# Four states of a selective scan: one scanned in PSUM, one on DVE and three on POOL multiplied by C, the sums over the states as matmuls with an identity

## The chip, the cores and the metric

The kernel runs on one core of one Trainium2 chip. The metric is the device time of one execution in microseconds (us). Before the change it is 11720.34 us, the median of three runs (11690.25 to 11727.8).

The engines are named as the profile names them: PE is TensorE's matmul, PEld its weight load, DVE is VectorE, ACT is ScalarE, POOL is GpSimd, SP is SyncE, which issues the DMAs. PE, DVE, ACT and POOL each run their instructions in the order in which the program wrote them.

## What is computed

An image batch of shape (4, 64, 64, 96) passes through four layers. Layers 0 and 1 are two-dimensional selective scans (1 works on the Fourier transform of the image), layers 2 and 3 are attention and a quantized feed-forward network over tokens. The scans take nearly all of the time. For each of four directions k, each channel d and each of 16 states n, along the sequence l:

```
delta = softplus(dt_w @ dts + dt_b)            # per direction, channel, position
h[d,n]  = h[d,n] * exp(delta[d] * A[d,n]) + delta[d] * u[d] * B[n]
y[d]    = sum_n h[d,n] * C[n]  + Ds[d] * u[d]
y_out   = y_0 + flip(y_2) + transpose(y_1 + flip(y_3))
```

Then `y_out` is layer-normalized, gated with silu(z) and projected. B and C depend on the position but not on the channel; delta and u depend on the channel but not on the state.

## The kernel before

**Tiling.** Channels lie on the 128 partitions, the sequence on the free axis. Each block of layers has C = 3 chunks of 128 channels. Layer 0 (`CFG0`) packs two images with 64 channels each into a chunk (NI = 2, PI = 64); its two image pairs are two phases. Layer 1 (`CFG1`) has one image and 128 channels per chunk (NI = 1, PI = 128), so four phases. Each direction of a phase is cut into segments: eight of 512 positions in layer 0, and 512, 512, 384, 384 and 320 in layer 1. That gives 64 segments in layer 0 and 80 in layer 1. A segment is done in 12 steps: for q in 0..3 (four states each) and c in 0..2 (chunk). So there are 768 steps in layer 0 and 960 in layer 1.

**One step** (the loop from L763) makes four scans on DVE (`scan`, L660, `tensor_tensor_scan`): state 0 and 1 of the four go to the tile `hx`, state 2 and 3 to `hy`. Their coefficients exp(delta*A) are made by ACT (`exp`, L635): for states 0 and 1 into SBUF (`ax`, `front_x`), for 2 and 3 into PSUM (`front_y`). The inhomogeneous term delta*u*B comes in two ways. For states 0 and 1, ACT scales the transposed delta*u by B, one number per partition (`make_bx`, L600), and PE transposes the result back into PSUM (`transposed`, L630). For states 2 and 3, POOL multiplies delta*u by a B that a DMA has spread over all partitions (`front_b`, L653, tile `hy`). The products with C are made by POOL for `hx` (L805, both states in one instruction of 2S elements, S being the segment's length) and by DVE for `hy` (L822, both states in one instruction). The sum over the states is made by PE: `accumulate` (L682) transposes each 128x128 block of each product into the accumulator `acc` with `is_transpose=True`, so that the sum lies with positions on the partitions. `keep_state` (L673) keeps the last column of each scan for the next segment: POOL for `hx`, mostly ACT for `hy`.

**PSUM** has eight banks: three accumulators, three "ab" rooms, through which the four PSUM tiles of a step (two transposed B terms, two exps) rotate, one bank "pp" for the preparation of the next segment, one bank "ms" for all side work.

**Order.** Scans run under a manual schedule. In the gaps (`slot`, three a step) `prepare` (projections, softplus, transposes of the next segment) and a queue of side tasks (`E.step`: the convolution and projections of the next phase, the gating of the last one) are advanced a piece at a time; `rate` (1.75 to 2.5 pieces a step) limits the side tasks. `burst` places softplus and silu. So a matmul that waits on PE holds all matmuls behind it, the scan's and the side tasks'.

**After a segment,** `close_chunk` copies `acc` (ACT) and stores it to DRAM, positions first. `gated` (from L352) reads the four directions back, two rows of the image at a time, and adds them in PSUM: three plain matmuls with the diagonal of the summed Ds (`skip`, L397) and twelve transposes (L403) for each two rows.

## Time and profile before

The profiled execution has a span of 11704.4 us, 0.14% under the median of the runs (11720.34 us).

| | |
|---|---|
| span of the profiled execution | 11704.4 us |
| median of the runs | 11720.34 us (11690.25 to 11727.8) |
| busy: PE / PEld | 9301.7 (79%) / 6722.3 us |
| busy: DVE | 10549.4 us (90%) |
| busy: ACT | 9089.0 us (78%) |
| busy: POOL | 8931.5 us (76%) |
| mean granted PE clock | 0.880 |
| DMA | 1469.07 MB, 126 GB/s, queue share 45.5% |
| head before the first scan / stretch of the scans / tail | 0 to 218, 218 to 11313, 11313 to 11704 us |

The busy share of an engine is time in which at least one of its instructions was in flight. For PE this is more than the time that its array was needed: consecutive matmuls overlap, and a single one is shown for some 0.27 us although the next can start 0.11 us later. So the work of PE is better counted by the distance from the start of one instruction to the start of the next, where nothing holds them. The groups of instructions give, for a line and a shape, the count, the busy time, the mean duration of one, and what the engine waited for before them; a plain fp32 matmul is two instructions in them, a transposing one is one.

### The profile page before, as it was taken

The page shows a single profiled execution, that of the slowest core. Times are in us where ns is not written, and L with a number is a line of the kernel's source. Part 1 is how long each engine was busy: PE and PEld are TensorE (multiplying, and loading weights), DVE is VectorE, ACT ScalarE, POOL GpSimd, SP SyncE. Part 2 cuts the span into 40 slices and gives each one's busy share as a digit, 9 for nine tenths or more (in the row PEclk, how much of TensorE's full clock was granted, in tenths as well). Part 3 has the DMA queues.
Part 4 walks back from the last instruction along what each step waited for, and adds up shares of the span by engine and source line. Part 5 has one row for each costly group of instructions (what it writes and reads, how often), then busy time and mean ns, then how long its engine had stood idle before and what let it go on. Part 6 is the DMA issues. An engine that isn't in the chain of part 4 may idle for free. (4 is left out here: it accounts for less than half of the span.)

```text
span 11704.4 us, 164864 instructions
## 1 busy us (share of the span) xinstructions
PE 9301.7 (79%) x54800; PEld 6722.3 (57%) x54800; DVE 10549.4 (90%) x10183; ACT 9089.0 (78%) x18533; POOL 8931.5 (76%) x7075
## 2 busy tenths in 40 slices
PE   6678888787888878877888888888778877788765
PEld 3455555555666556555665565565556655565554
DVE  6899999999999998999888989988999999899974
ACT  3778888898888888887767878877787787777753
POOL 2889999887887897897768878877767767677640
PEclk8789999988988998998889989988879988898887
DMA  5454454555555445445544353454225432443242
GB/s 145 120 142 119 126 127 115 141 155 158 153 153 129 124 124 141 120 127 162 153 129 124 114 147 120 142 150 119 88 79 158 122 96 92 124 137 106 83 117 42
DMA packets 1270879, 1469.07 MB, mean 126 GB/s; under 512 B 496071, under 2 KB 1033871, under 8 KB 1260679
## 3 DMA queue, kind: packets, MB, share of 16 engines
q1 hardware_dynamic: 1270023, 1458.53, 45.5%
q8 instruction: 430, 7.05, 0.3%
q14 instruction: 426, 3.49, 0.1%
HBM read 1221.74 MB, written 236.50 MB: 125 GB/s over the span
## 5 line engine op out<-in xcount | busy, mean ns | idle before, releaser
L653 POOL TENSOR_TENSOR hy_l<-du_l,bc_l 128x512 f32<-128x512 f32 (+2 forms) x3456 | 3957.3, 1166 | 1934.8 <-DVE hcy_l L822 960.1
L805 POOL TENSOR_TENSOR hcx_l<-hx_l,bc_l 128x1024 f32<-128x1024 f32 (+2 forms) x1617 | 3525.5, 2180 | 239.1 <-DVE hx_l L660 197.9
L600 ACT ACTIVATE bx_l<-dut_l,bt_l 128x192 f32<-128x192 f32 (+2 forms) x6272 | 2793.7, 498 | 0.0
L682 PE MATMUL acc_l<-ident,hcx_l 128*128 128x128 f32 (+1 forms) x12006 | 1876.0, 305 | 392.6 <-POOL hcx_l L805 388.4
L635 ACT ACTIVATE ax_l<-delta_l,l_alog 128x512 f32<-128x512 f32 (+2 forms) x3456 | 2139.1, 667 | 0.0
L682 PE MATMUL acc_l<-ident,hcy_l 128*128 128x128 f32 (+1 forms) x12000 | 1841.9, 302 | 302.4 <-DVE hcy_l L822 299.0
L682 PEld LDWEIGHTS acc_l<-ident,hcy_l 128*128 128x128 f32 (+1 forms) x12000 | 1551.5, 155 | 859.2 <-DVE hcy_l L822 475.7
L682 PEld LDWEIGHTS acc_l<-ident,hcx_l 128*128 128x128 f32 (+1 forms) x12006 | 1526.4, 156 | 861.5 <-POOL hcx_l L805 665.9
L822 DVE TENSOR_TENSOR hcy_l<-hy_l,bc_l 128x1024 f32<-128x1024 f32 (+2 forms) x1616 | 1951.1, 1207 | 43.6
L660 DVE TENSOR_TENSOR_SCAN hx_l<-ax_l,state_l,b_l 128x512 f32<-128x512 f32 (+2 forms) x1650 | 1787.4, 1124 | 212.7 <-PE b_l L630 136.9
L660 DVE TENSOR_TENSOR_SCAN hy_l<-b_l,state_l,hy_l 128x512 f32<-128x512 f32 (+2 forms) x1649 | 1782.9, 1118 | 89.3 <-ACT b_l L635 81.4
L635 ACT ACTIVATE b_l<-delta_l,l_alog 128x512 f32<-128x512 f32 (+2 forms) x1913 | 1196.6, 628 | 627.6 <-DVE hx_l L660 599.0
L630 PE MATMUL b_l<-ident,bx_l 128*128 128x128 f32 (+1 forms) x6724 | 1169.6, 302 | 363.0 <-DVE hy_l L660 203.5
L635 ACT ACTIVATE ab_l<-delta_l,l_alog 128x512 f32<-128x512 f32 x1321 | 907.1, 689 | 547.5 <-DVE hx_l L660 496.4
L630 PEld LDWEIGHTS b_l<-ident,bx_l 128*128 128x128 f32 (+1 forms) x6724 | 827.1, 152 | 861.3 <-DVE hy_l L660 337.1
L660 DVE TENSOR_TENSOR_SCAN hy_l<-ab_l,state_l,hy_l 128x512 f32<-128x512 f32 x961 | 1172.1, 1257 | 60.8 <-POOL hy_l L653 31.9
L660 DVE TENSOR_TENSOR_SCAN hx_l<-ax_l,state_l,ab_l 128x512 f32<-128x512 f32 x962 | 1176.5, 1263 | 49.3 <-PE ab_l L630 27.3
L630 PE MATMUL ab_l<-ident,bx_l 128*128 128x128 f32 x5288 | 889.1, 305 | 383.2 <-DVE hy_l L660 206.3
L673 POOL COPY state_l<-hx_l 128x2 f32<-128x2 f32 x1344 | 1141.9, 850 | 0.0
L630 PEld LDWEIGHTS ab_l<-ident,bx_l 128*128 128x128 f32 x5288 | 652.0, 154 | 715.6 <-DVE hy_l L660 326.6
L274 PE MATMUL pc_l<-pad_l,l_dg 128*128 128x512 f32 (+2 forms) x1656 | 787.9, 564 | 56.0 <-ACT uh_l L252 46.6
L176 PE MATMUL pi_l<-xi_l,l_wi 96*128 96x384 f32 (+6 forms) x912 | 458.6, 619 | 180.0 <-ACT zh_l L342 60.4
(225 smaller groups left out, 11821.3 us busy)
## 6 DMA issues: line engine op xcount, KB each, us to landing
bc_l<-l_xd_l SPq DMA_DIRECT2D x1536, 256.0 KB
bc_l<-l_xd_l SPq DMA_DIRECT2D x384, 512.0 KB
bc_l<-l_xd_l SPq DMA_DIRECT2D x384, 384.0 KB
us_l<-l_u SPq DMA_DIRECT2D x96, 768.0 KB
l_y<-y_l SPq DMA_DIRECT2D x288, 256.0 KB
bc_l<-l_xd_l SPq DMA_DIRECT2D x192, 320.0 KB
yt_l<-l_y SPq DMA_DIRECT2D x264, 192.0 KB
yt_l<-l_y SPq DMA_DIRECT2D x128, 384.0 KB
```

Source lines behind the costliest of these rows:

```text
L176: self.nc.tensor.matmul(out[i * cfg.PI : (i + 1) * cfg.PI, :n], wi[:, ki, half, :], xin[:, max(i, ki), :n], start=(ki == 0), stop=(ki == c ...
L274: nc.tensor.matmul(pc[:, : n * 64].rearrange("p (r w) -> p r w", w=64), diag[:, t, :], pad[:, r - p0 + dy : r - p0 + dy + n, dx : dx + 64] ...
L600: nc.scalar.activation(t[:n, b, :, ch], z.dut[:n, b, :, ch], AF.Copy, scale=z.bt[:n, b, m : m + 1])
L630: nc.tensor.transpose(pb[:, t : t + n], st.z.bx[st.q, j][:n, b, st.c], ident[:n, :n])
L635: nc.scalar.activation(out, z.delta[:, st.c, : z.S], AF.Exp, scale=z.blk.A[:, st.c, z.k, n : n + 1])
L653: nc.gpsimd.tensor_tensor(st.hy[:, j, :S], st.z.du[:, st.c, :S], st.z.b[st.q][:, j, :S], ALU.mult)
L660: nc.vector.tensor_tensor_scan(h[:, j, : z.S][:, ::step], a[:, : z.S][:, ::step], b[:, : z.S][:, ::step], 0.0 if z.first else z.state[st.c ...
L673: copy(z.state[st.c][:, n0 : n0 + 2].rearrange("p (j o) -> p j o", o=1), h[:, :, e : e + 1])
L682: nc.tensor.matmul(z.acc[st.c][:n, b, :], hc[:, j, t : t + n], ident, start=(n0 + j == 0 and b == 0), stop=(n0 + j == NST - 1 and b == 0), ...
L805: nc.gpsimd.tensor_tensor(hcx[:, :, :S], hx[:, :, :S], z.c[q][0][:, :, :S], ALU.mult)
L822: nc.vector.tensor_tensor(hcy[:, :, :S], st.hy[:, :, :S], z.c[q][1][:, :, :S], ALU.mult)
```

## The change

Of the four states of a step, 0 and 1 still get their B term through PE (`made` = 2), but in another way; state 0 is now scanned in place in PSUM (`kept` = 1), states 1 to 3 in an SBUF tile `h`.

- **B by matmuls.** ACT no longer scales delta*u but an identity (`make_diagonals`: one activation of 128x128 for each block, image and state). PE multiplies the transposed delta*u by this diagonal (`spread_b`): a plain matmul for each block of 128 positions and each image, so two of half width per block in layer 0.
- **Products with C.** DVE multiplies state 0 alone (`multiply_kept`, S elements, from PSUM), ACT keeps its last column. POOL multiplies the three others in one instruction of 3S elements and keeps their last columns in one copy (`multiply`), one step later than before.
- **Sums.** `add` is a plain matmul of the whole segment against the identity, four a step, one at once (`add_kept`) and three a step later (`add_rest`). So `acc` stays channels-first. Directions 0, 2 and 3 add one more term per chunk (`fetch_more`): the skip term for direction 0, the stored sum of direction 0 or 1 for directions 2 and 3.
- **Stores and gating.** Sums are stored channels-first; `gated` reads two arrays, one as it lies, and one crossed (rows and columns exchanged) in loads of up to 17 rows, and adds both by plain identity matmuls over a whole row block.
- **Broadcasts.** B rows and C rows are fetched separately, C as four rows in one load and one step later than B.

The diff, cut to its core:

```diff
+CFG0 = Cfg("l0", ..., 1e-5, 2, 1)      # made, kept
+CFG1 = Cfg("l1", ..., 1e-5, 2, 1)
...
-    def make_bx(z, q):
+    def make_diagonals(z, q):
...
-                        t[:n, b, :, ch], z.dut[:n, b, :, ch], AF.Copy, scale=z.bt[:n, b, m : m + 1]
+                        t[:n, b, i, j, :n], ident[:n, :n], AF.Copy, scale=z.bt[:n, b, m : m + 1]
...
-    def transposed(st, j):
-        pb = room(st, j)
-        for b, (t, n) in enumerate(st.z.blocks):
-            nc.tensor.transpose(pb[:, t : t + n], st.z.bx[st.q, j][:n, b, st.c], ident[:n, :n])
-        return pb
+    def spread_b(st, j):
+        z, PI = st.z, st.z.cfg.PI
+        pb = st.px[j] = room(st, j)
+        for b, (t, n) in enumerate(z.blocks):
+            for i in range(z.cfg.NI):
+                ch = slice(i * PI, (i + 1) * PI)
+                nc.tensor.matmul(
+                    pb[ch, t : t + n], z.dut[:n, b, st.c, ch], z.dg[st.q][:n, b, i, j, :n], start=True, stop=True
+                )
...
+    def multiply_kept(st):
+            nc.vector.tensor_tensor(hk[:, : z.S], st.px[j][:, : z.S], z.c[st.q][:, j, : z.S], ALU.mult)
+                nc.scalar.copy(z.state[st.c][:, n : n + 1], st.px[j][:, e : e + 1])
+    def multiply(st):
+        nc.gpsimd.tensor_tensor(st.hc[:, :, :S], st.h[:, :, :S], z.c[st.q][:, kept:, :S], ALU.mult)
+            nc.gpsimd.tensor_copy(... st.h[:, :, e : e + 1])
...
-                nc.tensor.matmul(z.acc[st.c][:n, b, :], hc[:, j, t : t + n], ident, ..., is_transpose=True)
+    def add(st, w, v, first=False, final=False):
+        nc.tensor.matmul(st.z.acc[st.c][:, : st.z.S], w, v[:, : st.z.S], start=first, stop=final)
...
             scan(st, 0)
+            for j in range(made, 3):
+                front_y(st, j)
             if nxt:
                 front_x(nxt)
+            multiply_kept(st)
+            front_y(st, 3)
             long = burst()
+            if before:
+                multiply(before)
+            if nxt:
+                front_b(nxt)
+            add_kept(st)
             slot(None)
             scan(st, 1)
+                spread_b(nxt, 0)
             scan(st, 2)
+            if before:
+                add_rest(before)
             slot(None, hold=long)
+                spread_b(nxt, 1)
             scan(st, 3)
             slot(LATE)
-            nc.vector.tensor_tensor(hcy[:, :, :S], st.hy[:, :, :S], z.c[q][1][:, :, :S], ALU.mult)
+            before = st
```

## The prediction, on record before the result

> **What bounds the kernel now.** I read the page first (busy shares, groups), then busy time by stretch, then the time line. The page: DVE is busiest; L822 is the DVE multiply that shrinks, L805 the POOL multiply that grows.
>
> ```profile
> PE 9301.7 (79%) x54800; PEld 6722.3 (57%) x54800; DVE 10549.4 (90%) x10183; ACT 9089.0 (78%) x18533; POOL 8931.5 (76%) x7075
> ...
> L805 POOL TENSOR_TENSOR hcx_l<-hx_l,bc_l 128x1024 f32<-128x1024 f32 (+2 forms) x1617 | 3525.5, 2180 | 239.1 <-DVE hx_l L660 197.9
> ...
> L822 DVE TENSOR_TENSOR hcy_l<-hy_l,bc_l 128x1024 f32<-128x1024 f32 (+2 forms) x1616 | 1951.1, 1207 | 43.6
> ```
>
> Stretches: the first two layer 0 phases, one of layer 1, the tail. Columns: length, busy of PE, PEld, DVE, ACT, POOL, then granted clock.
>
> ```profile
> 218.00:2773.00 2555.00, 1970.83 (x10875) 1359.14 (x10876) 2422.38 (x1994) 2169.31 (x4490) 2269.26 (x1647) 0.89 0.50 131
> 2773.00:5359.00 2586.00, 2098.84 (x12844) 1592.18 (x12843) 2436.31 (x2042) 2179.61 (x4536) 2213.66 (x1598) 0.90 0.53 137
> ...
> 8275.00:9798.00 1523.00, 1203.85 (x7257) 874.96 (x7258) 1427.09 (x1578) 1179.55 (x2435) 1080.10 (x932) 0.86 0.36 107
> ...
> 11313.00:11704.00 391.00, 235.64 (x1626) 180.71 (x1624) 139.81 (x262) 129.45 (x325) 2.73 (x4) 0.74 0.39 84
> sum 11486.00, PE 9176.71 PEld 6673.45 DVE 10435.61 ACT 9036.75 POOL 8926.77; mean PE 1310.96 PEld 953.35 DVE 1490.80 ACT 1290.96 POOL 1275.25
> ```
>
> In the scans' 11095 us DVE is busy 10435.61 - 139.81 = 10296, or 93%: DVE bounds it, everywhere. Layer 0 takes 5141 us (6.69 a step), layer 1 5954 (6.20).
>
> The time line of PE shows what its instructions really cost: from start to start.
>
> ```profile
> 3364.00 1.04 PE L630 MATMUL b_l<-ident,bx_l 128*128 128x128 f32 x8
> 3364.87 1.02 PE L428 MATMUL pv_l<-sq_l,l_mean_w 128*128 128x512 f32 x2
> 3365.73 1.07 PE L682 MATMUL acc_l<-ident,hcx_l 128*128 128x128 f32 x8
> ```
>
> Eight 128-column transposes take 0.87 us, 0.109 each; one plain fp32 matmul of 512 columns (two instructions) 0.86. Per 512 columns: transpose 0.435, plain 0.86. Half-width matmuls:
>
> ```profile
> 8005.28 0.82 PE L682 MATMUL acc_l<-ident,hcx_l 128*128 128x128 f32 x6
> 8006.03 1.18 PE L1026 MATMUL piv<-ih,at 128*64 128x64 f32 x16
> 8007.14 0.87 PE L682 MATMUL acc_l<-ident,hcy_l 128*128 128x128 f32 x6
> ```
>
> Sixteen instructions (two output halves by turns) last 1.18 with some 0.28 of the last one's latency: 0.12 a pair. Six transposes should hand over after 0.65, not 0.75: 0.1 lost at the change of width.
>
> **PE, the path.** Work at full clock, in us, over the scans:
> - Now: 38016 transposes (528 blocks of positions in all segments x 72) x 0.109 = 4144. Preparation: six plain matmuls, 12 full and 4 small transposes a segment, 6.7 x 96, 5.05 x 32 and 4.3 x 16 = 874, say 880. Side matmuls (convolution L274 570, projections L176 360, Fourier, gating and output projections the rest), each group's columns at 0.84 ns a pass: 1780. Sum 6800.
> - Sums: four a step plus 324 extra terms = 4824 of 512 columns, 1608 of 384, 804 of 320: x 0.86, 0.645, 0.54 = 5620.
> - B terms, layer 0: 6144 pairs x 2 passes x 0.12 = 1475. Bounds 1327 (columns alone, 0.108) and 2666 (no overlap, 0.217).
> - B terms, layer 1: 6528 matmuls x 0.217 = 1417.
> - Width changes: 4 a step x 768 x 0.1 = 307; bounds 0 and 460.
> - Gating: about 2300 transposes and skip instructions out (250), 108 pairs of plain matmuls in (160 to 320): taken as -60.
>
> After: 6800 - 4144 + 5620 + 1475 + 1417 + 307 - 60 = 11415 in a stretch that now lasts 11095. Layer 0: 7.47 a step, against 6.69 in all today; layer 1: 5.91 against 6.20. PE becomes the bound.
>
> The clock: 0.86 to 0.90 by stretch, but it follows PE's own load.
>
> ```profile
> 1509.00:1639.00 130.00, 110.01 (x628) 70.40 (x628) 127.62 (x108) 115.99 (x246) 124.22 (x86) 1.00 0.48 124
> 1700.00:1740.00 40.00, 29.45 (x150) 22.93 (x149) 39.36 (x32) 33.00 (x68) 38.59 (x33) 0.74 0.52 121
> ```
>
> 85% busy had 1.00, 74% had 0.74. So a PE that never rests gets the full clock, and I take the work undivided; at 0.89 it would be 12826. [...]
>
> **The other engines, beside PE.**
> - DVE loses L822 (1951 in the group shown, 2055 with its small ones) and gains 1728 multiplies of one state with a PSUM operand. The nearest row is L421, 128x512 from PSUM, 673 ns; scaled, 1067. DVE falls to 9310. Scanning into PSUM has no row; scans that read PSUM cost 1257 to 1264 ns whichever operand lies there, so I take 0, neither gain nor loss; at 0.6 us each (1040, half a scan) DVE would still be under PE.
> - POOL: 1024 elements 2363 ns, 768 1818: 2.13 ns an element and 0.18 fixed. So 1536 cost 3.45, 1152 2.64, 960 2.23, in all 5416, against 3716. Its state copies cost 1252 now, mostly waiting beside DVE's multiply:
>
> ```profile
> 3001.12 0.20 POOL L673 COPY state_l<-hx_l 128x2 f32<-128x2 f32 x1
> 3001.30 1.22 DVE L822 TENSOR_TENSOR hcy_l<-hy_l,bc_l 128x1024 f32<-128x1024 f32 x1
> ...
> 3007.26 1.31 DVE L822 TENSOR_TENSOR hcy_l<-hy_l,bc_l 128x1024 f32<-128x1024 f32 x1
> 3007.41 1.19 POOL L673 COPY state_l<-hx_l 128x2 f32<-128x2 f32 x1
> ```
>
>   Begun inside the multiply, a copy ends with it (3008.60 and 3008.57). The new multiply reads PSUM and one SBUF tile, so this may go. 1440 copies: 260 (at 0.18) to 1224 (at 0.85). POOL: 9635 to 10600, second, hidden under PE.
> - ACT: 6272 diagonals of 128 elements at 388 ns (from 442 for 192 and 603 for 384) replace 2794 by 2434. Hidden. Its copy of an accumulator comes one step before PE wants that bank again: 0.57 us under a cover of some 7. If a softplus burst (1.49 and two table loads of 1.28, 4 us, once a segment) stood there each time, 144 x 4 = 576; it is within what I allow for waits.
> - Weight loads (PEld) take 0.11 to 0.16 us an instruction and overlap: under a pass of 0.43 they vanish, under one of 128 columns they stand as today.
> - SP and DMA: broadcasts carry the same bytes in 1664 issues instead of 2496; C is fetched one step later, two steps (13 us) ahead of use; 1 MB at the mean 126 GB/s takes 8. If that cover went, DVE's first multiply of a quarter would wait, and PE behind it. The crossed loads (14 in the scans, 64-byte pieces) arrive some seven steps before their matmul; lower bound 0, upper 11 us each (the longest wait for a flip's load, L306), 160; I take 40.
>
> **Waits on PE, in order.** The sum of state 0 waits for DVE's multiply; the first B term for scan 1 (its room); the three late sums for POOL, whose multiply begins when the previous step ends, four or five microseconds before; the second B term for scan 2. Behind each stand all later matmuls, side tasks too, and DVE's next scans wait for those. In a step without side work the first B term is ready about 0.5 us before scan 1 is; steps with it have none. Also the one "ms" bank makes PE wait for ACT's copies (L397 for yb 80, L176 for zh 60 us today); that was free and now is not. I take the share that today's bound reaches, 0.928: 11415 / 0.928 = 12300. With head and tail (218 + 391, unchanged; the tail's crossed load and lighter merge within 20 either way) and 40: 12949 against the profiled execution's own 11704. The median lies 16 above: **12965**.
>
> **Rivals.**
> - Halves of the B terms don't overlap: 1191 more work, 12606 / 0.928 + 665 = 14250. Against it: the 16 instructions in 1.18. One weight load per pass in between (0.16 a pair) would give 13500.
> - PE waits more: 0.86 of the stretch, by late C, three rooms for four tiles or a clock under 1: 13940.
> - PE waits next to nothing: 11415 + 609 + 16 = 12040.
> - Faster: a plain identity sum costs PE what a transpose does, 0.43 for 512 columns. Then PE has 8605, POOL bounds with 9635 to 10600, and the time is 11050 to 12090, middle 11400. It decides from 0.68 us a sum on, where PE's work falls to 10260 and the time to today's. Against it: every plain fp32 group has two instructions a matmul.
>
> **Numbers.** Forecast 0.63, halves 0.08, more waiting 0.13, next to no waiting 0.06, cheap sums 0.10 (0.07 faster, 0.02 the same, 0.01 slower). Under 0.3% a measurement here can't tell from no change. Faster 0.07, same 0.02, slower 0.91. The range leaves out the cheap sums and the halves' far end: 12000 to 13950.
>
> **What would show it.** L713 two instructions of 0.43 a 512-column sum; PE work per step 7.5 in layer 0; granted clock near 1; DVE waiting for PE before scans 0 and 1; POOL's copies near 0.2; layer 0 losing some 1040 us, layer 1 some 160. Wrong if PE is not the busiest, if L713 shows one pass, or if DVE's scans lengthen with PSUM output.

## The result, and the profile after

The changed kernel takes 14321.58 us (median of four runs, 14314.05 to 14328.35) against 11708.32 us (11690.25 to 11727.8) of the kernel before on the same chip: a ratio of 1.2227, with a 95% interval of 1.2204 to 1.2249. The forecast was 12965 us in a range of 12000 to 13950. The direction was right, the size was not: the loss is 2613 us where 1245 were forecast, and the time lies above the range.

The page of the kernel after, its engines and the lines that answer L805 and L822 of before, with DVE's scans that wait for PE (L676 is the scan, L713 the sum, L694 DVE's multiply, L705 POOL's, L639 the B term):

```profile
PE 12989.8 (91%) x66944; PEld 7433.0 (52%) x66944; DVE 10212.5 (71%) x10183; ACT 8416.3 (59%) x18616; POOL 9960.1 (70%) x6920
...
L705 POOL TENSOR_TENSOR hc_l<-h_l,bc_l 128x1536 f32<-128x1536 f32 (+2 forms) x1728 | 5574.9, 3226 | 3564.6 <-DVE h_l L676 2032.0
...
L676 DVE TENSOR_TENSOR_SCAN h_l<-ax_l,state_l,b_l 128x512 f32<-128x512 f32 (+2 forms) x885 | 990.7, 1119 | 1355.0 <-PE b_l L639 1250.7
...
L676 DVE TENSOR_TENSOR_SCAN h_l<-ax_l,state_l,ab_l 128x512 f32<-128x512 f32 x555 | 709.4, 1278 | 806.1 <-PE ab_l L639 755.2
...
L713 PE MATMUL acc_l<-hk_l,ident 128*128 128x512 f32 x1420 | 799.6, 646 | 267.5 <-DVE hk_l L694 266.6
```

PE is now the busiest, DVE waits for it before scan 1 (1250.7 and 755.2 us in these two groups), and PE waits for DVE's multiply. DVE has lost only 337 us of busy time, although its multiply L822 of 2055 us gave way to one of 1105.

The stretches of the kernel after, by phase: length, busy of PE, PEld, DVE, ACT, POOL, then the granted clock, the share of DMA and GB/s:

```profile
212.90:3236.70 3023.80, 2880.41 (x17119) 1462.48 (x17120) 2203.44 (x1992) 2043.93 (x4529) 2419.41 (x1600) 0.99 0.46 117
3236.70:6524.50 3287.80, 3113.78 (x18660) 1650.52 (x18659) 2262.47 (x2042) 2070.10 (x4572) 2406.48 (x1561) 0.97 0.46 109
...
10239.60:12145.30 1905.70, 1644.15 (x7380) 1028.15 (x7379) 1505.30 (x1560) 1058.67 (x2395) 1298.55 (x917) 0.93 0.31 88
...
13937.70:14317.00 379.30, 234.31 (x1391) 153.66 (x1389) 142.95 (x264) 130.54 (x325) 8.55 (x6) 0.77 0.24 58
```

Layer 0 takes 6312 us (5141 before, 6181 forecast), layer 1 takes 7413 (5954 before, 6114 forecast). So layer 0 came out within 131 us of the forecast; nearly all of the error, some 1300 us, is in layer 1. And there is a stretch of it (10239.6 to 12145.3) in which DVE is busy for longer than it was in the same phase before, 1505 us against 1427.

Step times in the tables below are the mean distance from the start of one step's DVE multiply (L694; L822 of before) to the next one's, read from the trace. "Side work" of DVE is the sum of the durations of its instructions other than scans and that multiply, between the first and the last scan of a layer. A variant without a range was run once; the runs of the kernel before in all these comparisons lie between 11686 and 11730 us.

### The profile page after: what moved, and what is told of

Read it like the earlier page. It is cut to its first block, busy times and chain, and to the rows that moved or that the text cites. A ratio compares the mean times of both kernels' runs of the same rounds, so it can differ in the third digit from the quotient of the medians.

```text
span 14317.1 us, 188500 instructions
## 1 busy us (share of the span) xinstructions
PE 12989.8 (91%) x66944; PEld 7433.0 (52%) x66944; DVE 10212.5 (71%) x10183; ACT 8416.3 (59%) x18616; POOL 9960.1 (70%) x6920
## 3 DMA queue, kind: packets, MB, share of 16 engines
q14 instruction: 420, 3.44, 0.1%
## 5 line engine op out<-in xcount | busy, mean ns | idle before, releaser
L705 POOL TENSOR_TENSOR hc_l<-h_l,bc_l 128x1536 f32<-128x1536 f32 (+2 forms) x1728 | 5574.9, 3226 | 3564.6 <-DVE h_l L676 2032.0
L713 PE MATMUL acc_l<-hc_l,ident 128*128 128x512 f32 (+2 forms) x10368 | 4552.6, 577 | 26.9 <-POOL hc_l L705 26.9
L665 POOL TENSOR_TENSOR h_l<-du_l,bc_l 128x512 f32<-128x512 f32 (+2 forms) x3456 | 4038.2, 1189 | 204.7 <-DVE du_l L564 66.3
L713 PEld LDWEIGHTS acc_l<-hc_l,ident 128*128 128x128 f32 x10368 | 1906.6, 198 | 1615.0 <-issue 1325.2
L639 PEld LDWEIGHTS b_l<-dg_l,dut_l 128*64 128x64 f32 (+2 forms) x21024 | 1786.7, 159 | 1126.9 <-issue 464.1
L639 PE MATMUL b_l<-dg_l,dut_l 128*64 128x128 f32 (+2 forms) x21024 | 2116.1, 286 | 143.4 <-DVE h_l L676 140.9
L606 ACT ACTIVATE dg_l<-ident,bt_l 128x128 f32<-128x128 f32 (+1 forms) x6272 | 2038.7, 390 | 26.5 <-PE ab_l L639 13.1
L676 DVE TENSOR_TENSOR_SCAN h_l<-b_l,state_l,h_l 128x512 f32<-128x512 f32 (+2 forms) x1772 | 1897.2, 1104 | 139.0 <-ACT b_l L645 128.6
L676 DVE TENSOR_TENSOR_SCAN h_l<-ax_l,state_l,b_l 128x512 f32<-128x512 f32 (+2 forms) x885 | 990.7, 1119 | 1355.0 <-PE b_l L639 1250.7
L639 PEld LDWEIGHTS ab_l<-dg_l,dut_l 128*64 128x64 f32 (+1 forms) x16608 | 1395.7, 160 | 894.8 <-issue 452.8
L639 PE MATMUL ab_l<-dg_l,dut_l 128*64 128x128 f32 (+1 forms) x16608 | 1605.5, 282 | 109.9 <-DVE h_l L676 107.1
L676 DVE TENSOR_TENSOR_SCAN h_l<-ab_l,state_l,h_l 128x512 f32<-128x512 f32 x1108 | 1356.7, 1261 | 49.0 <-ACT ab_l L645 43.0
L676 DVE TENSOR_TENSOR_SCAN h_l<-ax_l,state_l,ab_l 128x512 f32<-128x512 f32 x555 | 709.4, 1278 | 806.1 <-PE ab_l L639 755.2
L713 PE MATMUL acc_l<-k_l,ident 128*128 128x512 f32 (+2 forms) x2036 | 988.6, 568 | 317.3 <-DVE k_l L694 315.6
L676 DVE TENSOR_TENSOR_SCAN b_l<-ax_l,state_l,b_l 128x512 f32<-128x512 f32 (+2 forms) x885 | 990.6, 1119 | 371.0 <-PE b_l L639 364.1
L713 PE MATMUL acc_l<-hk_l,ident 128*128 128x512 f32 x1420 | 799.6, 646 | 267.5 <-DVE hk_l L694 266.6
L676 DVE TENSOR_TENSOR_SCAN ab_l<-ax_l,state_l,ab_l 128x512 f32<-128x512 f32 x555 | 708.0, 1276 | 161.3 <-PE ab_l L639 157.0
```

The costliest lines, as they stand in the source:

```text
L606: nc.scalar.activation(t[:n, b, i, j, :n], ident[:n, :n], AF.Copy, scale=z.bt[:n, b, m : m + 1])
L639: nc.tensor.matmul(pb[ch, t : t + n], z.dut[:n, b, st.c, ch], z.dg[st.q][:n, b, i, j, :n], start=True, stop=True)
L665: nc.gpsimd.tensor_tensor(st.h[:, j - kept, :S], z.du[:, st.c, :S], z.b[st.q][:, j - made, :S], ALU.mult)
L676: nc.vector.tensor_tensor_scan(h[:, ::step], a[:, ::step], b[:, ::step], 0.0 if z.first else z.state[st.c][:, n : n + 1], ALU.mult, ALU.add,)
L705: nc.gpsimd.tensor_tensor(st.hc[:, :, :S], st.h[:, :, :S], z.c[st.q][:, kept:, :S], ALU.mult)
L713: nc.tensor.matmul(st.z.acc[st.c][:, : st.z.S], w, v[:, : st.z.S], start=first, stop=final)
```

## The experiments

**Where the loss comes from: order, amount of work, or the rest of the change.** The first three variants keep the change and touch one cause each; the fourth undoes both of the parts that put plain matmuls on PE (B terms and sums are transposes again, stores and gating as before), and keeps the rest: state 0 scanned in PSUM, one state multiplied by DVE, three by POOL a step later, the new order. (For room in SBUF, two of its double buffers are single: DVE's product and the preparation's `xs`.)

Late sums behind the second B term:

```diff
-            if before:
-                add_rest(before)
             slot(None, hold=long)
             if nxt:
                 spread_b(nxt, 1)
             scan(st, 3)
+            if before:
+                add_rest(before)
```

> The three late sums are issued after the second B term instead of before it; nothing else changes. Theory 1 (order): PE's work was about right (5.6 to 7.2 us a step), and layer 1's 7.5 to 7.9 us a step are waits between queues that run in order: the second B term stands behind three sums and side matmuls, DVE's scan 1 waits for it, and PE then waits for DVE's multiply. It expects layer 1 at 6.4 to 7.0 us a step instead of 7.72, layer 0 at 7.6 to 8.1 instead of 8.22, in all 13100 to 13800 us. Theory 2 (work): PE simply has that much to do, order is nothing: 14200 to 14400. Theory 3 (ACT's order): the late exp of state 2 is what DVE waits for: 14100 to 14400.

13975.9 us: 345 us less, where theory 1 expected 520 to 1220. Layer 0 came down from 8.22 to 7.94 us a step, as it said, but layer 1, where it looked for the loss, only from 7.72 to 7.59 (6.4 to 7.0 expected). The order costs something; it isn't the cause of layer 1's error.

The exponential of state 2 written at the end of the step before:

```diff
-            for j in range(made, 3):
-                front_y(st, j)
+            if i == 0:
+                front_y(st, 2)
...
             scan(st, 3)
+            if nxt:
+                front_y(nxt, 2)
```

> The exp of state 2 is issued on ACT at the end of the step before instead of after scan 0, ahead of ACT's diagonals and of the copies that wait for PE. Theory 3 (ACT's order) expects 13700 to 14000 us, all of it in layer 1. Theory 1 (order on PE) expects 14100 to 14350, since scan 1, ahead of the scan that needs this exp, goes on waiting for PE. Theory 2 (work): 14300.

14422.9 us, 101 more. The order on ACT isn't the cause.

Two of the three late sums left out:

```diff
-        for j in range(many):
+        for j in range(many - 1, many):
             add(st, ident, st.hc[:, j], final=(st.q == NQ - 1 and j == many - 1))
```

> Two of the three late sums of each step are left out, so the output lacks states 1 and 2 of each four. PE has 2680 us less to do (2304 matmuls at 0.86, 768 at 0.645, 384 at 0.54), 1.72 a step in layer 0 and 1.42 on the mean in layer 1. Theory 2 (work) expects just that: layer 0 at 6.5 us a step, layer 1 at 6.3, in all 11640. Theory 1 (order) expects layer 0 at 6.5 too, and layer 1 to lose more than what was taken out, since the second B term comes earlier and the waits go: 5.7 to 6.1, in all 11050 to 11450.

12901.5 us. Neither: some 2680 us of PE work less (two sums of four by the forecast's prices, without the extra terms) bring only 1420, or 0.53 us for each us. PE's work is on the path, but something else comes up behind it: of the 1260 us that did not come, the trace shows some 860 as more idle time of PE, and some 340 as a slower clock (more on both below).

Both PE parts undone:

```diff
-        for b, (t, n) in enumerate(z.blocks):
-            for i in range(z.cfg.NI):
-                nc.tensor.matmul(pb[ch, t : t + n], z.dut[...], z.dg[...], start=True, stop=True)
+        for b, (t, n) in enumerate(st.z.blocks):
+            nc.tensor.transpose(pb[:, t : t + n], st.z.bx[st.q, j][:n, b, st.c], ident[:n, :n])
...
-        nc.tensor.matmul(st.z.acc[st.c][:, : st.z.S], w, v[:, : st.z.S], start=first, stop=final)
+            nc.tensor.matmul(acc[:m, b, :], v[:, t : t + m], ident, ..., is_transpose=True)
```

> The change without its two parts on PE: B terms by scaled delta*u and transposes, sums by transposing matmuls, stores and gating as in the kernel before; scan of state 0 in PSUM, DVE's multiply of one state, POOL's of three and the step order as in the changed kernel. (The tiles for state 0's product and for the projection's result have one buffer instead of two, for room.) PE's work is 6800 us again, POOL's 9950 and DVE's some 9500 by the changed kernel's groups. If PE's plain matmuls are the whole loss: POOL bounds, 10700 to 11300 us, faster than the kernel before. If the new split of work or the new order costs by itself (PE and ACT behind DVE's multiply, POOL's three states): 11700 to 12500.

12342.9 us (12339.5 to 12346.0), a ratio to before of 1.0542 (1.0524 to 1.0561). So the part of the change that was to relieve DVE loses 630 us by itself, with PE at its old load:

```profile
PE 9249.8 (75%) x54800; PEld 6948.8 (56%) x54800; DVE 10202.7 (83%) x10183; ACT 9026.1 (73%) x18688; POOL 9965.2 (81%) x6920
```

DVE is at 10202.7 us here too. The forecast's 9310, for the scans alone, makes some 9560 with DVE's 253 us of head and tail. The time line of the changed kernel shows why:

```profile
3362.01 2.84 PE L713 MATMUL acc_l<-hc_l,ident 128*128 128x512 f32 x6
3362.28 5.24 DVE L443 SCALAR_TENSOR_TENSOR yb_l<-yb_l,l_lnb,zb_l 128x512 f32<-128x512 f32 x3
...
3362.51 3.80 POOL L705 TENSOR_TENSOR hc_l<-h_l,bc_l 128x1536 f32<-128x1536 f32 x1 [2.13 <-DVE h_l L676]
...
3364.78 1.09 PE L639 MATMUL ab_l<-dg_l,dut_l 128*64 128x128 f32 x16
...
3368.75 0.69 DVE L694 TENSOR_TENSOR hk_l<-ab_l,bc_l 128x512 f32<-128x512 f32 x1
...
3369.59 0.89 PE L713 MATMUL acc_l<-hk_l,ident 128*128 128x512 f32 x1 [3.72 <-DVE hk_l L694]
```

Three instructions of the gating's layer norm, 0.73 us each where nothing hinders them, take 5.24 us. The first runs at once (0.73 us); the second starts 0.41 us after POOL's multiply and lasts 3.93, to 0.55 us after POOL's end. DVE's scan and multiply come late by that, and PE waits 3.72 us for the sum. Over the whole kernel the 15 instructions at L443 that met no POOL instruction took 652 ns in the mean (segments of 512, 384 and 320 columns together), the 93 that did 1689; of the 16-bit instructions at L1263 (token layers), 48 took 351 ns and 144 took 1284. It mattered there which of the two began first: of L443's instructions of 512 columns, the 22 that began while POOL's multiply L705 ran took 3556 ns in the mean, the 19 in which that multiply began 727. Up to 3.3 us fell on one instruction (L1282, 0.53 us at its quickest, 3.83 at its slowest). DVE's scans and its multiply L694, which read one operand from PSUM, kept their times: at 512 columns those that began while L705 ran took 1269 and 692 ns in the mean, those that met no L705 1256 and 692.

This was taken up as theory 4, on both kernels.

One state on POOL, both PE parts undone:

```diff
-        nc.gpsimd.tensor_tensor(st.hc[:, :, :S], st.h[:, :, :S], z.c[st.q][:, kept:, :S], ALU.mult)
+        nc.gpsimd.tensor_tensor(st.hc[:, 0, :S], st.h[:, 0, :S], z.c[st.q][:, kept, :S], ALU.mult)
...
-            add(st, st.hc[:, j - kept], 4 * st.q + j)
+            add(st, st.hc[:, 0], 4 * st.q + j)
```

> The kernel with both PE parts undone, but GpSimd multiplies only one of its three states (the sums read that product three times; the other two products are left out), so its instruction falls from 3.53 us to about 1.2. Theory 4 (while a GpSimd multiply runs, a VectorE instruction with two SBUF inputs or 16-bit ones stands still): VectorE's side work in layer 1 falls from 1119 us to 700 to 800, the last two phases from 7.2 us a step to 6.3 to 6.5; in layer 0, where GpSimd had 6.3 of 6.7 to 6.95 us a step, VectorE's 6.2 is left: together 11450 to 11850. Rival, the new order or ScalarE's state copy is the cause: layer 1 stays at 7.2 and the time above 12150.

11690.8 us beside 11729.7 of before: 652 us less, all that this part of the change had lost. DVE's side work in layer 1 falls from 1090 to 784 us (the expectation has 1119 for the first, by another count), the last two phases to 6.55 and 6.66 us a step, layer 0 from 6.70 and 6.95 to 6.36 and 6.63. The time lies in the range of theory 4; the rival (order, ACT's copy) falls.

The multiply in three instructions, both PE parts undone:

```diff
-        nc.gpsimd.tensor_tensor(st.hc[:, :, :S], st.h[:, :, :S], z.c[st.q][:, kept:, :S], ALU.mult)
+        for j in range(4 - kept):
+            nc.gpsimd.tensor_tensor(st.hc[:, j, :S], st.h[:, j, :S], z.c[st.q][:, kept + j, :S], ALU.mult)
```

> The kernel with both PE parts undone, GpSimd's multiply of three states cut into three instructions of one. Nothing is left out. Theory 4, standing still behind one instruction: the stretched VectorE work waits for at most 1.3 us instead of 3.5, so its side work in layer 1 falls from 1119 to 800 to 900 us and the last two phases to 6.5 to 6.9; GpSimd itself costs some 0.3 us a step more, at most 250 us in layer 0: 11950 to 12350 together. Rival, GpSimd's amount of work counts and not its instruction's length: 12400 to 12600 with unchanged side work.

12170.9 us, 172 less, with all the work done and POOL busy for 10443.9 us, 479 more. DVE's side work in layer 1 is 892 us, the last two phases take 6.75 and 6.74. Both the length of POOL's instruction and its amount of work count, in different places. In layer 1 the shorter instructions alone bring 0.26 us a step of the 0.42 that one state brought. In layer 0, where POOL's instructions fill some 6.3 of 6.8 us a step, they cost 0.10 (6.87 and 6.98), and one state gains 0.33.

One state on POOL, PE's work as changed (the edit of the variant with one state above, in the changed kernel):

> The changed kernel with all its PE work, GpSimd multiplying one of its three states (its product is summed three times, two products are left out). If PE alone sets the time: 14200 to 14330. Theory 4 beside PE's work: VectorE's side work in layer 1 falls from 1102 to 700 to 800 us and the three late sums come ready earlier, so layer 1 falls by 0.3 to 0.7 us a step and layer 0 by 0.2 to 0.4: 13500 to 13900.

13919.3 us: 402 less, just above the range. Layer 1 gains 0.10, 0.28, 0.57 and 0.34 us a step, layer 0 only 0.14 and 0.08. DVE's groups by shape, kernel before, kernel after, the split multiply without PE parts, and this one; the two lines are the 16-bit instruction of the token layers and the layer norm's last one:

```profile
L1211 DVE TENSOR_SCALAR h<-h,b 128x512 f16<-128x512 f16 x192 | 64.9, 377 | 14.2 <-ACT h L1208 10.7
...
L440 DVE SCALAR_TENSOR_TENSOR yb_l<-yb_l,l_lnb,zb_l 128x512 f32<-128x512 f32 x72 | 51.7, 770 | 0.0
```

```profile
L1263 DVE TENSOR_SCALAR h<-h,b 128x512 f16<-128x512 f16 x192 | 193.1, 1051 | 7.9 <-ACT h L1260 4.6
...
L443 DVE SCALAR_TENSOR_TENSOR yb_l<-yb_l,l_lnb,zb_l 128x512 f32<-128x512 f32 x72 | 117.7, 1689 | 0.0
```

```profile
L1259 DVE TENSOR_SCALAR h<-h,b 128x512 f16<-128x512 f16 x192 | 128.7, 714 | 8.0 <-ACT h L1256 4.7
...
L441 DVE SCALAR_TENSOR_TENSOR yb_l<-yb_l,l_lnb,zb_l 128x512 f32<-128x512 f32 x72 | 85.8, 1242 | 0.0
```

```profile
L1263 DVE TENSOR_SCALAR h<-h,b 128x512 f16<-128x512 f16 x192 | 103.0, 580 | 8.9 <-ACT h L1260 5.5
...
L443 DVE SCALAR_TENSOR_TENSOR yb_l<-yb_l,l_lnb,zb_l 128x512 f32<-128x512 f32 x72 | 74.4, 1087 | 0.0
```

The mean of one goes 377, 1051, 714, 580 ns and 770, 1689, 1242, 1087 ns. In the three with the new order it follows the length of POOL's instruction (3.55, three of 1.31, 1.27 us). The kernel before has 2.36 us and the lowest means, since DVE seldom meets POOL there: 42 of the 192 16-bit instructions ran beside one of POOL's multiplies, 144 in the kernel after. By the table of step times (us, six phases; two of layer 0, four of layer 1) the loss with the PE parts undone is greatest where the side work of the token layers runs, in the last two:

| | | | | | | |
|---|---|---|---|---|---|---|
| before | 6.65 | 6.73 | 6.13 | 6.02 | 6.35 | 6.33 |
| PE parts undone | 6.70 | 6.95 | 6.36 | 6.33 | 7.20 | 7.18 |
| the same, one state on POOL | 6.36 | 6.63 | 6.07 | 6.10 | 6.55 | 6.66 |
| the same, POOL's multiply in three | 6.87 | 6.98 | 6.24 | 6.29 | 6.75 | 6.74 |
| after | 7.88 | 8.56 | 7.80 | 7.68 | 7.94 | 7.50 |
| after, one state on POOL | 7.73 | 8.48 | 7.70 | 7.40 | 7.37 | 7.16 |

The sums undone, with the stores and the gating that belong to them (as in the fourth variant, the B terms left as plain matmuls):

> The changed kernel with its sums undone (transposes as before, and the stores and gating that go with them), B terms by diagonals kept. By my count 2857 us of PE work less, of the 4675 that the two PE parts add. If PE's work counts, whichever part it is: 14320 less 2857/4675 of the 1980 us between the two kernels, 13050 to 13200. If the sums count more, since scans and their late products meet there: 12500 to 12900. If the B terms do (scans wait for them directly): 13400 to 14000.

12796.9 us. That makes a ladder, in this order, from before: 630 us for the split of the products and its order, 454 for the B terms by diagonals, 1525 for the sums with their stores and gating. The sums count more than their share of PE's work, 77% of the two where my count of work has 61%.

**Why a us of PE's work costs what it does.** The side tasks were taken out of the steps, so that a step can be seen by itself:

```diff
-RATES = [1.75, 2.35, 2.5, 2.5, 2.5, 2.5]
+RATES = [0.0] * 6
```

> The changed kernel with the rate of the side tasks at zero: they run in a block where a segment of the next phase needs them, not inside the steps; preparation stays in the steps. Nothing is left out. The total says little (the side work no longer overlaps, 14300 to 15800); what counts is the step without side work. Theory 5 (each step lasts as long as the longer of PE's and VectorE's work in that step, since neither can run ahead; side work of one engine at a time makes the sum): the median step falls to the larger of both engines' own work, 6.2 to 6.7 us at 512 columns of layer 0, 4.9 to 5.4 at 384. Rival, the loop through the three rooms (the first B term waits for the room of scan 1, the late sums stand between the two B terms): 7.1 or more at 512 and 5.9 or more at 384.

15797.5 us in all, 6.74 us the median step of 512 columns in layer 0, 4.96 the one of 384: just above and within the range of theory 5; the rival's 7.1 and 5.9 fall. The time line of this variant, one step of layer 0 from B term to B term:

```profile
985.85 1.09 PE L639 MATMUL ab_l<-dg_l,dut_l 128*64 128x128 f32 x16
...
986.88 1.13 PE L541 MATMUL pp_l<-xs_l,l_dtw 76*128 76x512 f32 x2
987.06 1.28 DVE L676 TENSOR_TENSOR_SCAN h_l<-ax_l,state_l,ab_l 128x512 f32<-128x512 f32 x1 [1.20 <-PE ab_l L639]
...
987.84 1.02 PE L713 MATMUL acc_l<-hk_l,ident 128*128 128x512 f32 x2
...
988.79 1.09 PE L639 MATMUL ab_l<-dg_l,dut_l 128*64 128x128 f32 x16
...
989.82 2.84 PE L713 MATMUL acc_l<-hc_l,ident 128*128 128x512 f32 x6
...
992.59 1.09 PE L639 MATMUL ab_l<-dg_l,dut_l 128*64 128x128 f32 x16
```

Read from start to start, PE has no gap: 1.03 (B term), 0.96 (a matmul of the preparation), 0.95 (sum of state 0), 1.03, 2.77 (three late sums), 6.74 in all. Without the preparation it is 5.78; the forecast had 3.44 + 1.92 + 0.4 = 5.76. DVE waits 1.20 us in this step and in the next two, before scan 1. That is its whole reserve.

DVE's multiply cut to 64 columns (the two tiles that PE sums are kept and only their first 64 columns are written anew):

```diff
-            nc.vector.tensor_tensor(hk[:, : z.S], st.px[j][:, : z.S], z.c[st.q][:, j, : z.S], ALU.mult)
+            nc.vector.tensor_tensor(hk[:, :64], st.px[j][:, :64], z.c[st.q][:, j, :64], ALU.mult)
```

> The changed kernel, in which VectorE multiplies only 64 of a state's columns by C (the rest of that product is left out; PE sums the whole tile as before). Takes some 0.55 us a 512-column step, 880 us in all, from VectorE and from the way between scan 0 and the first sum. If PE alone sets the time: less than 120 us gained, 14200 or more. If the two engines set it by turns: a third to two thirds of it, 13700 to 14050.

14216.7 us: 105 gained of the 717 that left DVE.

```profile
L695 DVE TENSOR_TENSOR hk<-b_l,bc_l 128x64 f32<-128x64 f32 x1014 | 227.7, 225 | 34.7
L695 DVE TENSOR_TENSOR hk<-ab_l,bc_l 128x64 f32<-128x64 f32 x714 | 160.4, 225 | 27.3 <-DMA bc_l<-l_xd_l 2.9
```

By this, PE sets the regular step, as forecast, and the other expectation (the engines by turns, DVE's work counting a third to two thirds) falls: DVE's regular work is covered by that reserve. What isn't covered are its blocks of 2 to 5 us. The longest waits of PE, in the kernel after and in the one with one state on POOL (total, times, longest):

```profile
PE acc_l L713 <- DVE k_l L694: 315.6, 135, 8.2
PE acc_l L713 <- DVE hk_l L694: 266.6, 100, 8.5
```

```profile
PE acc_l L713 <- DVE k_l L694: 204.8, 119, 6.1
PE acc_l L713 <- DVE hk_l L694: 172.1, 95, 5.6
```

In the kernel after 235 waits make 582 us, 2.5 us each: rare and long, not a little in every step. Shorter blocks give 205 us of it back.

A wait goes with a loss beyond its length: stretches at half clock follow such waits. In the kernel after, layer 1, DVE first, then PE, then the stretch from 7107.5 us on with its granted clock (0.50):

```profile
7101.83 4.02 DVE L443 SCALAR_TENSOR_TENSOR yb_l<-yb_l,l_lnb,zb_l 128x512 f32<-128x512 f32 x3
```

```profile
7101.56 1.88 PE L713 MATMUL acc_l<-hc_l,ident 128*128 128x320 f32 x6
...
7107.17 1.14 PE L713 MATMUL acc_l<-k_l,ident 128*128 128x320 f32 x2 [2.92 <-DVE k_l L694]
...
7113.88 3.57 PE L713 MATMUL acc_l<-hc_l,ident 128*128 128x320 f32 x6
```

```profile
7107.50:7117.70 10.20, 10.20 (x30) 6.91 (x28) 3.09 (x5) 2.77 (x7) 4.29 (x4) 0.50 0.40 135
```

A layer-norm block holds DVE up, PE waits 2.92 us for the product, and for the next 10.2 us it works without a gap at half the clock: three late sums take 3.57 us instead of 1.88. Over the kernel, the two instructions of a 512-column sum start 429 ns apart at full clock and 854 at half. Layer 1 has 149 such stretches, 5.6 us long in the mean; in the 5 us before one, PE stood idle for 2.6 us, against 0.5 in an average 5 us of the layer. That the waits bring the clock down is read from this; no run set the clock by itself. What both cost in layer 1 (us; half of the time at work at half clock is lost):

| layer 1 | time | PE idle | half clock | PE at work in it |
|---|---|---|---|---|
| after | 7413 | 774 | 836 | 726 |
| late sums last | 7279 | 665 | 788 | 679 |
| DVE's multiply of 64 columns | 7322 | 738 | 700 | 619 |
| one state on POOL | 7104 | 590 | 502 | 451 |
| late sums last, POOL's multiply in three (next) | 7038 | 520 | 509 | 444 |

PE has the same work in all five, and the differences come out of the two columns: one state on POOL brings 309 us, 184 of them idle time and 138 half of the work at half clock.

Both small gains together, late sums last and the multiply in three:

> The changed kernel with the late sums behind the second B term and GpSimd's multiply in three instructions, nothing left out. The first gave 345 us alone, the second 172 where PE was light. If they are separate losses: 13750 to 13900. If the split only helps where VectorE is the longer engine: 13900 to 14000.

13706.1 us, 615 less than the changed kernel and below the range of separate losses: 345 for the order, and 270 more for the split (from 13975.9), 241 of them in layer 1. So the split gains more beside PE's work than the 172 without it. This is the best form of the change that was run, with all its work, and is 17% over the kernel before.

The kernel before with its POOL multiply in two instructions:

```diff
-            nc.gpsimd.tensor_tensor(hcx[:, :, :S], hx[:, :, :S], z.c[q][0][:, :, :S], ALU.mult)
+            for j in range(2):
+                nc.gpsimd.tensor_tensor(hcx[:, j, :S], hx[:, j, :S], z.c[q][0][:, j, :S], ALU.mult)
```

> The kernel before with GpSimd's multiply of two states cut into two instructions. Theory 4 at work there too, only smaller: the instruction that forms du (1962 ns where 1545 stood free of GpSimd, 96 of them) and some side work lose up to 60 us to GpSimd's 2.36 us; half of it comes back: 11670 to 11720 against 11710, hardly to be told from no change. If GpSimd's longer total (0.2 us a step more) meets a wait of VectorE: 11750 to 11850.

11827.9 us, a ratio of 1.0100 (1.0083 to 1.0117): 1% slower, beyond the spread of the runs: the second case, though not by the wait named there. (In the kernel before, the 10 instructions of 1536 columns that form du and met no POOL instruction took 1734 ns in the mean, not 1545; the other 86 took 1988.) The two multiplies of DVE, kernel before and this one:

```profile
L822 DVE TENSOR_TENSOR hcy_l<-hy_l,bc_l 128x1024 f32<-128x1024 f32 x1152 | 1510.2, 1311 | 32.1
```

```profile
L823 DVE TENSOR_TENSOR hcy_l<-hy_l,bc_l 128x1024 f32<-128x1024 f32 x1152 | 1586.1, 1377 | 32.2
```

L822 reads two SBUF tiles and takes longer beside POOL: in the kernel before, 233 of the 1152 met no POOL instruction and took 1220 ns in the mean, the 919 that met one 1334. POOL's work became 0.2 us longer a step (two instructions of 1275 ns for one of 2363), and all these multiplies together grew from 2054 to 2148 us, 94 of the 112 lost. So cutting POOL's instruction helped DVE's side work (1090 to 892 us in layer 1, with the PE parts undone) and hurt the multiply, most of whose instructions meet POOL.

**What ties PE and DVE together.** Three more variants without side work in the steps. Four rooms in PSUM (the side tasks' bank):

```diff
-    E = Env(tc, lambda name: ps.tile([P, 512], F32, name=name, tag="ms"))
+    E = Env(tc, lambda name: ps.tile([P, 512], F32, name=name, tag="pp"))
...
-        return ps.tile([P, 512], F32, name=f"ab_{st.nm}_{j}", tag="ab", bufs=3)
+        return ps.tile([P, 512], F32, name=f"ab_{st.nm}_{j}", tag="ab", bufs=4)
```

> As e9 (no side work in the steps), with four rooms in PSUM for B terms and exponentials instead of three (the bank comes from the side tasks, which share the preparation's). If the rooms tie PE to VectorE: the median 512-column step of layer 0 falls from 6.74 us to 6.4 or less, the mean of the steps under 14 us from 6.96 to 6.6 or less, and the 384-column one from 4.96 to 4.85. If not: within 0.1 of e9's.

One state on POOL (the edit shown for it above, with the rates at zero):

> As e9, with GpSimd multiplying one of its three states (the other two products are left out). If GpSimd's 6.3 us sets the 512-column step of layer 0: its median falls from 6.74 to 6.3 to 6.45, and the 384-column one stays at 4.96. If not: 6.65 or more.

The late sums last (the first edit above, with the rates at zero):

> As e9, with the late sums behind the second B term. If PE's order (late sums between the two B terms) sets the step: the median at 512 columns of layer 0 falls from 6.74 to 6.5 or less. If not: within 0.1.

Medians of the 512-column step of layer 0 and means of the steps under 14 us (layer 0, layer 1): with none of these 6.74, 6.97, 5.78; four rooms 6.74, 6.81, 5.63; one state on POOL 6.74, 6.97, 5.77; late sums last 6.39, 6.53, 5.54. POOL's amount of work makes no difference without side work in the steps, though its instructions fill 6.1 us of 6.74. The rooms cost 0.15 us of the mean step and nothing of the median, which is between the two expectations. PE's order costs most: with the two B terms together PE changes its width twice a step instead of four times, and its B terms and sums start 1.90, 2.68 and 0.86 us apart, 5.44 instead of 5.78.

The kernel before without side work in the steps (the same edit of the rates):

> The kernel before with the rate of the side tasks at zero (as e9 for the changed one; nothing is left out, the total is longer since the blocks stand alone). If VectorE bounds the step there and hides PE's side work, only VectorE's own side work leaves the steps (0.14 us of 0.29 in layer 0, 0.63 of 0.76 in layer 1): the mean of the steps under 14 us is 6.5 to 6.7 in layer 0 (6.69 with side work) and 5.5 to 5.75 in layer 1 (6.20). Then the steps without side work are nearly as long in both kernels and the loss lies in the side work. If the step itself carries the loss: 6.2 or less and 5.2 or less.

6.26 us in layer 0 and 5.31 in layer 1, between the two cases. So both carry part of it. Means of the steps under 14 us, and the side work that the edit takes out of a step, counted from the instructions of both traces:

| us a step | layer 0 before | layer 0 after | layer 1 before | layer 1 after |
|---|---|---|---|---|
| without side work in the steps | 6.26 | 6.97 | 5.31 | 5.78 |
| with it | 6.62 | 8.09 | 6.18 | 7.62 |
| the side work makes | 0.36 | 1.12 | 0.87 | 1.84 |
| PE's side work taken out | 1.01 | 1.02 | 1.06 | 1.06 |
| DVE's side work taken out | 0.11 | 0.15 | 0.55 | 0.99 |

In the kernel before the side work costs DVE's share and a quarter to nearly a third of PE's. In the changed one it costs nearly the sum of both, 96% of it in layer 0 and 90% in layer 1. Of the 1.44 us that a step of layer 1 lost, 0.47 are in the step itself and 0.97 in the side work: 0.44 because DVE's share became longer, beside POOL's longer instruction, and some 0.5 because PE's is no longer hidden. This division is argued, not shown, and the clock is in it: with side work the changed kernel's steps of layer 1 hold 0.81 us of half clock, without it 0.11, which makes some 0.35 us of the 1.84.

What stays open is which resource keeps the one engine from making up, in steps without side work, for what the other held up. The rooms are worth 0.15 us where there is no side work; with it a fourth room wasn't tried: its bank is the one that the side tasks use.

## Why the prediction was wrong, by its steps

- **PE bounds, at the price of a plain fp32 matmul.** Right. L713 runs as two instructions of 0.43 us per 512 columns, halves of a B term overlap (16 instructions in 0.95 to 1.03 us), and the estimate of 0.1 for each of the four changes of width fits the sum (the step with two of them saves 0.34, more than 0.2, so they aren't the whole of that). The regular step of layer 0 has 5.78 us of B terms and sums for 5.76. Counted from the trace at the forecast's rates, with the 0.1 for each change of width, PE's work is 7.33 us a step in layer 0 (7.47 forecast) and 5.90 in layer 1 (5.91).
- **"I take the share that today's bound reaches, 0.928", on work at full clock.** This step failed. Work and step time give 7.33 / 8.22 = 0.89 in layer 0, but 5.90 / 7.72 = 0.76 in layer 1, and layer 1 alone accounts for 1300 us of the error. The share was DVE's, as the bounding engine: DVE's own blocks of side work are work in it. With PE as the bound, the same blocks make PE wait, and POOL's longer instruction stretched them from 0.69 to 1.11 us a step of layer 1. The forecast left 440 us of layer 1 for everything that isn't PE's work. The trace shows 774 us of idle time, 495 of them for DVE's multiply; some 360 lost to half clock, where the sum has nothing; and some 610 in which PE is in flight for longer than the counted work. What those 610 are stays open. Layer 0 came within 131 us partly by luck: its work was 108 us less than counted, its other losses 683 us where 445 were left for them.
- **"So a PE that never rests gets the full clock."** The condition did not hold: PE rests, rarely and long. The four phases of layer 1 were granted 0.95, 0.95, 0.93 and 0.94, those of layer 0 0.99 and 0.97. A clock under 1 stood only in a rival.
- **"DVE falls to 9310."** In the scans, for which the 9310 stands, it fell to 9957. The multiply was right (692 ns for 673), scanning into PSUM costs next to nothing (1276 for 1261 ns in the 512-column forms). The missed term is DVE's other work, taken as unchanged: in layer 1 it went from 661 to 1064 us, since what begins beside POOL's instruction of 3.55 us takes longer (the 48 of L1263 that began while L705 ran 2956 ns, where the 48 that met no POOL instruction took 351). The prediction had a case of it and read it one way only: its rows of POOL's copy, begun inside DVE's multiply and ending with it, were used for a gain of POOL (right: its copies take 206 ns, 850 before) and not turned round to ask which DVE work takes longer beside a POOL instruction half as long again.
- **"POOL ... second, hidden under PE."** Busy time right (9960 in 9635 to 10600), the conclusion wrong: 402 us of the time go away when POOL multiplies one state, 652 where PE is at its old load; with all the work done, shorter instructions bring 270 and 172.
- **Rivals.** "PE waits more", 0.86 and 13940 us, was the nearest, with 13 in 100. Of its causes the clock is one; the rooms were worth 0.15 us a step where that was tried; waits for C came to 12 us in all (POOL 11.1, DVE 0.9). It did not name DVE's blocks, and it stopped short. "Halves don't overlap", 14250, is near the time by chance; the rows refute it.
- **ACT, head and tail, crossed loads.** ACT is hidden at 8416; head and tail took 213 and 379 us. The 85 us that PE waited for the gating's loads fell on the array read as it lies (`yt`, L403), not on the crossed one. But the sum that reads the crossed one (L405) took 0.89 us an instruction of 512 columns where L713 takes 0.43, some 60 us in the scans. None of them matters.
- **The range.** Its upper end came from waits of 14% on PE. Adding DVE's stretched side work of layer 1 to PE's, 5.90 + 1.11 = 7.0 us a step, would have come nearer to the 7.72 measured, and still short of it.

No version that beats both kernels came up. The one without PE's parts and with little POOL work only draws level with the kernel before, and leaves out two products of three.

## What to carry to other kernels

When a change moves the bound from one engine to another, don't carry the old bound's share over: list the blocks of work on the engine that is relieved, compare them with the wait that it will have in a regular step (here 1.2 us), and count what is longer as a wait of the new bound. If that bound is PE, count the half clock behind such waits too; here the time lost to it in layer 1, 363 us, came to nearly half of the idle time itself, 774. And when an instruction on GpSimd grows, look at VectorE's instructions that can begin beside it. In the kernel after, four kinds took longer when they began during GpSimd's multiply, some by nearly its full length: the layer norm's with two SBUF tiles (L443, 0.75 us when free, 3.56 in the mean), the 16-bit ones (L1263, 0.35 and 2.96; L1282, 0.55 and 2.61), the token layers' sum of two tiles (L1286, 0.55 when free, 3.41 in the mean of 12) and a small one (L1184, 0.17 at its quickest, up to 3.33). Those with an operand in PSUM (L694, 0.69) and the reduction of one fp32 tile (L1183, 0.94) kept their times.

## What the runs showed of the hardware

- Some instructions of VectorE and GpSimd took longer beside one of the other engine, one by one and both ways. A layer-norm instruction of 0.73 us took 3.93, ending 0.55 us after GpSimd's multiply; a 16-bit one with a single SBUF tensor (L1263), 351 ns when free, took 1284 in the mean when it met GpSimd. GpSimd's copies in the kernel before took 955 ns in the mean when they began inside VectorE's multiply L822 (977 of them), 268 when they met none (406). In the kernel after, the 81 that began inside L694, with one operand in PSUM, took 188. VectorE's multiply with one operand in PSUM kept its time: L694 took 691 to 694 ns in all its 1152 instructions of 512 columns in the kernel after.
- Shorter GpSimd instructions for the same work aren't a remedy by themselves: 172 and 270 us gained in two kernels, 112 lost in a third, by what stands beside them.
- The granted clock was full or half, nothing between, in all records of both kernels' traces (369 stretches of half before, 202 after); in layer 1 of the kernel after, 836 of 7413 us were at half, 11%, with a mean of 0.94. There a stretch of half clock lasted 5.6 us in the mean, most of it with TensorE at work, and came after 2.6 us of idle time in 5.
